# Two-layer graph attention kernel: normalisations of phase A one step later, and the weight and token sums at the boundary shared out anew

## The chip, the cores and the metric

The kernel runs on one core of one Trainium2 chip. The metric is the device time of one execution in microseconds (us), taken as the median of several runs. A separate profiled execution gives the trace: its *span* is the time from the first to the last instruction of the program.

A core has five engines that run their own instruction queues and meet through semaphores: TensorE (PE in the profile, with its weight loads as PEld), VectorE (DVE), ScalarE (ACT), GpSimd (POOL) and SyncE (SP, which here issues all DMAs). Each queue is worked in the order in which the program wrote it.

## The reference, cut to what matters

The input is 128 graphs of 64 nodes with 768 features in float32. Two layers follow each other, each with a residual and a layer normalisation:

```python
# layer 0: gated graph attention with 12 heads of 64
h    = x @ W                       # per head
attn = softmax(mask(leaky(tanh(h) @ w_src + (tanh(h) @ w_dst).T)))
gate = sigmoid(x @ H_w.T + H_b)
x    = layernorm(x + gate * elu(attn @ h + b) + (1 - gate) * x)
# layer 1: masked attention with 6 heads of 128
q, k, v = x @ Wq + bq, x @ Wk + bk, x @ Wv + bv
x    = layernorm(x + softmax(q @ k.T / sqrt(128) + bias) @ v @ Wf + bf)
```

## The kernel before, in words

The 8192 rows make 64 tiles of 128 rows, two graphs each. Two tiles form a pair, and there are 32 pairs (`NP`). All large products are done with fewer multiplications by a scheme in the manner of Strassen: sums of blocks of the tokens and of the weights are made first, on VectorE or GpSimd, and TensorE then multiplies these.

**Phase A** does layer 0 and the product with Wv. A pair takes part in three products, W (for h), G (for the gate) and V (for v). Each consists of seven dense steps `i` = 0 to 6 of three matmuls (`Product.matmuls`, line 209), and after each step one eviction: steps 0, 2 and 3 copy the running sum to a `snap` buffer on ScalarE (line 418), steps 1, 4 and 5 add such a copy on VectorE (lines 441 and 460), step 6 copies on ScalarE (lines 439 and 458). TensorE may go on in the same accumulator only when the eviction has read it: step 4 needs the snap of step 2, step 5 that of step 3, step 6 the addition of step 4.

The order of all work is written out by hand. `at(step, ...)` appends a function to a list of events for a numbered step, and `run` calls them step by step. Within a step the order is that of the appending, where earlier pairs come first. Pair `p` begins at step `O[p]`: 0, 14, 28, and then every 21 steps. From there the attention of its two tiles follows in fixed distances. The object `Tile0(p, 1)` starts at `s = o`, `Tile0(p, 0)` five steps later. In what follows "30.0" is tile 0 of pair 30, and "W4.2" is dense step 2 of the product W of pair 4. The parts of a tile that matter here:

- `add` (ScalarE, line 532), `mask` and `top` (VectorE, lines 539 and 543), `exp` (ScalarE, line 548), `scale` (a reciprocal on VectorE, line 556, then a product on GpSimd, line 558): the softmax.
- `probs` (TensorE transposes, line 569, copied by ScalarE, line 574), `aggregate` (TensorE, line 587), `elu` (lines 608 and 615), `mix1` and `mix2` (VectorE, lines 620 to 630).
- `norm1` (step `s + 29`): statistics on VectorE, then 1/sqrt and a shift on GpSimd (lines 296 to 301). `norm2` (step `s + 30`): the normalisation itself on ScalarE (line 305), which waits for that shift. Only for the last pair is it done on VectorE (line 639). `spill` (step `s + 31`): SyncE stores the tile.
- `load(p)` (step `o + 8`) reads the pair's x into two of the four slots 0, 1, 5 and 6 of the buffer `xb`; the slots were those of pair `p - 2`.
- `x1_in` reads a spilled tile back in blocks, `x1T` transposes it on VectorE (line 397), `x1_sums` makes its token sums on GpSimd, and the product V follows. For the last pair `x1T` is done by TensorE (line 412).

**The boundary.** At the end of phase A the weights of layer 1 are prepared. Wq and Wk are loaded early into the buffers that W and H_w leave. Each needs 14 sums over slots of 128 x 512 elements (`WEIGHT_SUMS`, `weight15_sum`, line 167): VectorE makes those of Wq, GpSimd those of Wk, from step `o + 44` and `o + 45` of the last pair on, beside its V product.

**Phase B** does layer 1 for 16 groups of two pairs. A group first makes q and k for its heads in two halves `j`, in the order q0, k0, q1, k1. Each is a `Stream` of 15 steps (`STEPS`, `R` = 15) of two matmuls (line 876); the half `j` reads only columns `j * 128` to `j * 128 + 127` of each weight slot. ScalarE and VectorE collect the results (lines 897 and 902). The tokens' side needs 11 sums over the group (`SUMS`, `group_sum`, line 846, 128 x 512 each) of the transposed tokens `T4`, which lie in slots 1 to 4 of `xb`. For group 0 all are made on VectorE, four steps ahead of their use or, where that is not possible, before the first step. For group 1 six are made on VectorE and five on GpSimd, for later groups all on GpSimd. `dup` holds copies of four parts of group 0's tokens, made by ScalarE (line 1113), so that `T4` can be refilled. After q and k come scores, softmax, context (`load_v` brings v into slots 5, 6 and 0 of `xb`) and the product with Wf (steps F, from step 150 of the group). Wf is loaded in steps 2 to 7 of phase B, and its 14 sums are made by GpSimd from step 16 on. `load_adj` loads the mask of a group and has VectorE turn it into `fill` at once (line 811).

Of the kernel before, what the change touches and what calls it, by code (L numbers as in the profile page):

```python
# [9 lines left out]
F32 = mybir.dt.float32  # L10
# [51 lines left out]
def kernel(  # L62
# [99 lines left out]
        r = src.rearrange("(h p c) o -> h c p o", h=2, c=CH)  # L162
        return [r[k // CH, k % CH] for k in range(NC)]

    def weight15_sum(wb, k, eng):
        to, a, b, sign = WEIGHT_SUMS[k]
        eng.tensor_tensor(wb[:, to], wb[:, a], wb[:, b], SIGN[sign])

    def weight_sums(part, eng, ks=range(4)):

# [97 lines left out]


    T4 = xb[:, 1:5].rearrange("p (q i) (c n) -> p q i c n", q=2, n=P)  # L270

    def load_T4(g):
        for q in range(2):
# [34 lines left out]
    def phase_a(ctx):  # L308
# [342 lines left out]
        def at(step, *fs):  # L651
            events.setdefault(max(step, 0), []).extend(fs)

        def dense(d, key, i):
            d[key].matmuls(i)
            d[key].evict(i)
# [19 lines left out]
        for p in range(NP):  # L676
            d, o = st[p], O[p]
            d["p"] = p
            if p:
                at(max(o - 20, 1), lambda p=p: load_adj(p))  # L680
                at(o + 8, lambda p=p: load(p))

            def xb_in(d, i):
                d.setdefault("xp", []).append(blocks(x_t[2 * d["p"] + i]))

            def xT(d, i):
                d.setdefault("T", []).append(turn(d["xp"][i]))
# [12 lines left out]
            for i in range(7):  # L700
                at(o + i, lambda d=d, i=i: dense(d, "W", i))
                at(o + 7 + i, lambda d=d, i=i: dense(d, "G", i))
            for i, s in ((1, o), (0, o + (4 if p == NP - 1 else 5))):
                t = Tile0(p, i)
                at(s + 6 + (i == 0), t.tanh, t.cap)
                at(s + 7, t.dst_mul)
                at(s + 8, t.src_mul)
                at(s + 9, t.dst_sum, t.dst_out)
                at(s + 10, t.src_sum)
                at(s + 13, t.dst_in)  # L710
                at(s + 16, t.exchange)

                at(s + (15 if i else 17), lambda t=t: t.add(0))
                at(s + (16 if i else 17), lambda t=t: t.add(1))
                at(o + (14 if i else 16), t.gate_in)
                at(o + (17 if i else 18), t.gate)
                n = s - (i == 1)
                at(n + 18, t.mask, t.top)
                at(n + 19, lambda t=t: t.exp(0))
                at(n + 20, lambda t=t: t.exp(1))  # L720
                at(s + 21, lambda t=t: t.scale(0), lambda t=t: t.scale(1))
                at(s + 24, t.probs)
                at(s + 25, t.aggregate)
                at(s + 26, t.elu)
                at(s + 27, t.mix1)
                at(s + 28, t.mix2)
                at(s + 29, t.norm1)
                at(s + 30, t.norm2)
                at(s + 31, t.spill)

            def x1_in(d, i):
                d["xp", i] = blocks(x1_d[2 * d["p"] + i])

            def x1T(d, i, t):
                d["x1T", i] = t
                nc.sync.dma_start(xT_d[d["p"]][:, i], t)

            def x1_sums(d):
                d["T"] = [d["x1T", i] for i in range(2)]
                sums(d)  # L740

            if p < NP - 3:
                v = O[p + 3] + 14
                times = ((1, v - 19, v - 13), (0, v - 16, v - 10))
            elif p < NP - 1:

                v = O[-1] + (21 if p == NP - 3 else 28)
                times = ((1, v - 16, v - 7), (0, v - 15, v - 6)) if p == NP - 3 else (
                    (1, v - 12, v - 7), (0, v - 10, v - 6)
                )  # L750
            if p < NP - 1:
                for i, t0, t1 in times:
                    at(t0, lambda d=d, i=i: x1_in(d, i))
                    at(t1, lambda d=d, i=i: x1T(d, i, turn(d["xp", i])))
                at(times[1][2] + 1, lambda d=d: x1_sums(d))
            else:
                v = o + 45
                for i in range(2):
                    at(o + 43 - i, lambda d=d, i=i: x1T(d, i, transposed(d["x"][i])))
# [6 lines left out]
            at(4 + c, lambda c=c: weight_sums(lambda s: w1[:, s, c], nc.vector))  # L766


        o = O[-1]
        early = []  # L770

        def load_early(i, src, k):
            if k == 0:
                early.append(weight15(i))
            load15(early[i], src, k)

# [9 lines left out]
        return early  # L786


    def phase_b(ctx, wq, wk):
# [15 lines left out]
        def load_adj(g):  # L805
            d = st[g]
            a = small.tile([P, 2, 2, S], U8, name="adj1")
            for q in range(2):
                nc.sync.dma_start(a[:, q], adj_p[2 * g + q])
            d["fill"] = small.tile([P, 2, 2, S], F32, name="fill1")  # L810
            nc.vector.tensor_scalar(
                d["fill"], a, 1.0, -L1_NEG, op0=ALU.subtract, op1=ALU.mult
            )

        def load_v(g, q, i):
# [18 lines left out]
                nc.gpsimd.tensor_tensor(t, t, bf_bc, ALU.add)  # L834


        def group_part(d, r):

            if r < 6:
                return T4[:, :, r // 3, 2 * (r % 3) : 2 * (r % 3) + 2, :]  # L840
            return d["S"][r - 6]

        def group_sum(d, k, eng):
            r0, r1, op = SUMS[k]
            t = k1.tile([P, 2, 2, P], F32, name=f"S{k}")
            eng.tensor_tensor(t, group_part(d, r0), group_part(d, r1), op)  # L846
            d["S"][k] = t

        def pair_part(d, q, r):

# [217 lines left out]
        def at(step, *fs):  # L1068
            events.setdefault(max(step, 0), []).extend(fs)
# [4 lines left out]

        R = len(STEPS)
        N = 6 * R
        wf = weight15(2)
        for k in range(NC):
            at(2 + k, lambda k=k: load15(wf, Wf, k))
        for k in range(len(WEIGHT_SUMS)):  # L1080
            at(16 + 2 * k, lambda k=k: weight15_sum(wf, k, nc.gpsimd))
        for g in range(NG):
            d, o = st[g], N * g
            d["S"] = {}
# [5 lines left out]
            for k in range(len(SUMS)):  # L1090
# [19 lines left out]
                at(t, lambda d=d, k=k, eng=eng: group_sum(d, k, eng))  # L1110
# [114 lines left out]
```

## Time and profile before

| | |
|---|---|
| median of 3 runs | 2884.05 us (2882.27 to 2884.43) |
| the profiled execution's own time | 2882.71 us |
| its span | 2880.6 us |
| TensorE busy | 2825.0 us, 98% |
| VectorE busy | 1877.8 us, 65% |
| GpSimd busy | 1535.4 us, 53% |
| ScalarE busy | 1201.5 us, 42% |
| mean granted TensorE clock | 0.997 of full speed |

The 2.1 us between span and time lie around the program. A line of the timeline gives start, duration, engine, line of the kernel, operation and names (`out<-in`), the shape and how many instructions it merges; in brackets stand the idle time of the engine before it and what ended that idle time. Matmuls are recorded in pairs: a dense step of phase A is `x6`, one of a stream `x4`. Phase A lies from 0 to some 1470 us, phase B from 1475 us on.

### The profile page before, as it was taken

Reading aid. Unit: us, or ns where it says so; the run is one execution under the profiler, and the core shown is the slowest. Engines: PE = TensorE matmul, PEld = TensorE weight load, DVE = VectorE, ACT = ScalarE, POOL = GpSimd, SP = SyncE. Lnnn points to the kernel's source line nnn. Section 1 sums busy time; section 2 is a strip of 40 time slices with the busy share of each in tenths; the row PEclk is TensorE's granted clock in tenths of the full one; section 3 lists DMA queues with packets and bytes.
Section 4 is the critical chain, followed back from the end, with each engine's and each line's share of the span. In section 5 each row is a group of like instructions: output and inputs, shape, how many; then the busy total and the mean of one; then the engine's idle time right before and its main releaser. Section 6 shows DMA issues by size and latency. Waiting matters only on the chain.

```text
span 2880.6 us, 50750 instructions
## 1 busy us (share of the span) xinstructions
PE 2825.0 (98%) x18108; PEld 2061.9 (72%) x18108; DVE 1877.8 (65%) x3716; ACT 1201.5 (42%) x3737; POOL 1535.4 (53%) x1633
## 2 busy tenths in 40 slices
PE   8899999999999999999989999999999999999998
PEld 4556566666665665666558888888888888888887
DVE  4787777777877777778675555555555555555556
ACT  4656656566566565565522221222211222211223
POOL 4755655655555565555462555346454456454455
PEclk9999999999999999999999999999999999999999
DMA  6335445344454454443640211212211212211222
GB/s 179 108 107 155 126 134 150 116 146 137 124 146 137 124 155 122 139 143 121 201 147 18 89 69 59 84 56 89 89 65 58 89 56 89 89 61 62 89 83 72
DMA packets 358683, 308.40 MB, mean 107 GB/s; under 512 B 226592, under 2 KB 304160, under 8 KB 358432
## 3 DMA queue, kind: packets, MB, share of 16 engines
q1 hardware_dynamic: 358432, 305.16, 34.5%
q8 instruction: 144, 2.36, 0.3%
q14 instruction: 107, 0.88, 0.1%
HBM read 191.41 MB, written 101.06 MB: 102 GB/s over the span
## 4 chain that ended last, share of the span: by engine, by line
PE 86%; DVE 6%; POOL 3%; DMA 2%; issue 1%; ACT 1%; SPq 1%; DVEq 0%; POOLq 0%; ACTq 0%
PE X L876 42%; PE X L209 37%; PE pb L1016 2%; PE pb L941 2%; PE pa L587 2%; PE pa L569 1%; DVE z L629 1%; PE pb L996 1%; DVE z L620 1%; DVE S L846 0%; DVE w L173 0%; POOL th L490 0%; POOL w L173 0%; DVE st L284 0%; DVE xb L630 0%
## 5 line engine op out<-in xcount | busy, mean ns | idle before, releaser
L209 PE MATMUL X<-w,S 128*128 128x384 f32 x2304 | 800.8, 493 | 18.2 <-ACT snap L418 7.4
L876 PE MATMUL X<-S,w 128*128 128x256 f32 x2816 | 667.0, 383 | 7.2 <-DVE S L846 5.9
L209 PEld LDWEIGHTS X<-w,S 128*128 128x128 f32 x2304 | 430.6, 191 | 309.4 <-ACT snap L418 18.4
L209 PE MATMUL X<-w,T 128*128 128x384 f32 x1728 | 596.1, 487 | 6.0 <-ACT snap L418 3.5
L876 PEld LDWEIGHTS X<-S,w 128*128 128x128 f32 x2816 | 525.5, 190 | 82.2 <-DVE S L846 7.3
L209 PEld LDWEIGHTS X<-w,T 128*128 128x128 f32 x1728 | 326.1, 191 | 229.4 <-ACT snap L418 7.8
L858 POOL TENSOR_TENSOR Sc<-cT 128x256 f32<-128x256 f32 x224 | 161.7, 729 | 405.4 <-PE X L876 392.0
L876 PE MATMUL X<-w,Sc 128*128 128x256 f32 x1408 | 322.5, 381 | 0.9 <-DVE xs L919 0.8
L919 DVE TENSOR_TENSOR xs<-xs,X 128x256 f32<-128x256 f32 x512 | 210.6, 420 | 169.0 <-PE X L876 160.3
L876 PEld LDWEIGHTS X<-w,Sc 128*128 128x128 f32 x1408 | 265.4, 190 | 38.7 <-DVE xs L919 1.6
L548 ACT ACTIVATE s<-s,nmx 128x64 f32<-128x64 f32 x768 | 256.2, 335 | 76.8 <-DVE nmx L543 76.8
L902 DVE TENSOR_TENSOR k<-k,X 128x256 f32<-128x256 f32 x320 | 133.7, 421 | 216.0 <-PE X L876 166.1
L902 DVE TENSOR_TENSOR q<-q,X 128x256 f32<-128x256 f32 x320 | 133.2, 420 | 179.7 <-PE X L876 146.0
L305 ACT ACTIVATE xs<-xs,shift,rstd 128x768 f32<-128x768 f32 x62 | 63.5, 1025 | 419.0 <-POOL shift L301 412.4
L876 PE MATMUL X<-xb,w 128*128 128x256 f32 x960 | 236.6, 379 | 0.0
L897 ACT ACTIVATE k<-X,bk_c 128x256 f32<-128x256 f32 x192 | 91.1, 474 | 306.9 <-PE X L876 306.8
L897 ACT ACTIVATE q<-X,bq_c 128x256 f32<-128x256 f32 x192 | 91.1, 474 | 284.3 <-PE X L876 284.3
L482 POOL TENSOR_TENSOR tmp<-th,wd_bc 128x768 f32<-128x768 f32 x64 | 141.4, 2210 | 126.8 <-ACT th L478 126.8
L296 POOL TENSOR_TENSOR rstd<-rstd,neg_half 128x1 f32<-128x1 f32 x126 | 69.3, 550 | 247.4 <-DVE rstd L295 246.3
L532 ACT ACTIVATE s<-s,src 128x64 f32<-128x64 f32 x768 | 193.3, 335 | 15.0 <-DMA s<-dst_d 14.4
L876 PEld LDWEIGHTS X<-xb,w 128*128 128x128 f32 x960 | 181.2, 190 | 24.0
L418 ACT COPY snap<-X 128x384 f32<-128x384 f32 x288 | 134.8, 468 | 101.3 <-PE X L209 99.5
(119 smaller groups left out, 4110.3 us busy)
## 6 DMA issues: line engine op xcount, KB each, us to landing
xb<-in_x_dram SPq DMA_DIRECT2D x64, 384.0 KB
s<-dst_d SPq DMA_DIRECT2D x128, 192.0 KB
x_d<-xb SPq DMA_DIRECT2D x64, 384.0 KB
xT_d<-T SPq DMA_DIRECT2D x64, 384.0 KB
v_d<-v SPq DMA_DIRECT2D x128, 192.0 KB
xb<-xT_d SPq DMA_DIRECT2D x32, 768.0 KB
xb<-v_d SPq DMA_DIRECT2D x256, 96.0 KB
xs<-x_d SPq DMA_DIRECT2D x64, 384.0 KB
```

Source lines behind the costliest of these rows:

```text
L209: nc.tensor.matmul(o, self.lhsT(i, c), rhs, start=first and c == 0, stop=last and c == CH - 1, skip_group_check=True,)
L296: nc.gpsimd.tensor_tensor(rstd, rstd, neg_half, ALU.pow)
L305: nc.scalar.activation(r, r, AF.Identity, bias=shift, scale=rstd)
L418: nc.scalar.copy(t, ps)
L482: nc.gpsimd.tensor_tensor(self.tmp, self.th, wd_bc, ALU.mult)
L532: nc.scalar.activation(self.s[:, a], self.s[:, a], AF.Prelu, bias=self.src[:, a : a + 1], alpha=LEAKY_ALPHA,)
L548: nc.scalar.activation(self.s[:, a], self.s[:, a], AF.Exp, bias=self.nmx[:, a : a + 1], accum_out=self.sm[:, a : a + 1],)
L858: nc.gpsimd.tensor_tensor(t, pair_part(d, q, r0), pair_part(d, q, r1), op)
L876: nc.tensor.matmul(ps, self.lhsT(r, slot, c), self.rhs(r, slot, c), start=start and c == 0, stop=stop and c == 1, skip_group_check=True,)
L897: nc.scalar.activation(o[:, b], ps, AF.Identity, bias=bias[:, hd : hd + 1], scale=1.0 if positive else -1.0)
L902: nc.vector.tensor_tensor(o[:, b], o[:, b], ps, ALU.add if positive else ALU.subtract)
L919: nc.vector.tensor_tensor(o, o, ps, ALU.add if positive else ALU.subtract)
```

## The change

1. In phase A, `norm2` and `spill` of all pairs but the last come one step later. `load(p)` moves from `o + 8` to `o + 10`. `scale` of tile 1 is put at the front of its step. For pair 30, `x1_in` of tile 1 is one step earlier and both `x1T` (and the sums after them) one step later.
2. `weight15_sum` takes a range of columns. At the boundary VectorE makes only the first 128 of the 256 columns of each of the two blocks in a slot, so 128 x 256 elements a sum: all 14 of Wq in steps `o + 44` to `o + 47`, and the first 9 of Wk in `o + 49` to `o + 51`. Between them, at `o + 48`, it makes the first four group sums of group 0, into slots of `xb` that x has left (0, 5 and 6).
3. In phase B VectorE makes Wk's last five first halves in steps 8 to 12. GpSimd makes the first sum of Wf in step 8, then the second halves of Wq (steps 9 to 22) and of Wk (21 to 34), and the other 13 sums of Wf in steps 68 to 92. At the end of phase A GpSimd makes no weight sums any more.
4. Group 0's other seven sums stay on VectorE, in the order of their need, five steps ahead. Group 1's eleven sums are all on GpSimd, one step later than before.
5. The `fill` of a group is no longer made with the load of its mask, but in step 26 of the group.

```diff
-    def weight15_sum(wb, k, eng):
+    def weight15_sum(wb, k, eng, o=slice(0, 256)):
         to, a, b, sign = WEIGHT_SUMS[k]
-        eng.tensor_tensor(wb[:, to], wb[:, a], wb[:, b], SIGN[sign])
+        eng.tensor_tensor(wb[:, to, :, o], wb[:, a, :, o], wb[:, b, :, o], SIGN[sign])
...
+    free = [xb[:, 0], *(xb[:, 5:7].rearrange("p t (u n) -> p (t u) n", u=3)[:, 2 * k : 2 * k + 2] for k in range(3))]
+    EARLY = [free[0].rearrange("p (u n) -> p u n", u=3)[:, :2], *free[1:]]
+    EARLY = [t.rearrange("p q (c n) -> p q c n", n=P) for t in EARLY]
+    WK_EARLY = 9
...
+    def group_sum(d, k, eng, t):
+        r0, r1, op = SUMS[k]
+        eng.tensor_tensor(t, group_part(d, r0), group_part(d, r1), op)
+        d["S"][k] = t
...
+        def at_front(step, *fs):
+            events.setdefault(step, [])[:0] = fs
...
-                at(o + 8, lambda p=p: load(p))
+                at(o + 10, lambda p=p: load(p))
...
-                at(s + 21, lambda t=t: t.scale(0), lambda t=t: t.scale(1))
+                (at_front if i else at)(s + 21, lambda t=t: t.scale(0), lambda t=t: t.scale(1))
...
-                at(s + 30, t.norm2)
-                at(s + 31, t.spill)
+
+                n = s + (0 if p == NP - 1 else 1)
+                at(n + 30, t.norm2)
+                at(n + 31, t.spill)
...
-                    (1, v - 12, v - 7), (0, v - 10, v - 6)
+                    (1, v - 13, v - 6), (0, v - 10, v - 5)
...
-            at(o + 44 + k // 2, lambda k=k: weight15_sum(early[0], k, nc.vector))
-            at(o + 45 + k // 2, lambda k=k: weight15_sum(early[1], k, nc.gpsimd))
+            at(o + 44 + k // 4, lambda k=k: weight15_sum(early[0], k, nc.vector, slice(0, P)))
+        for k in range(4):
+            at(o + 48, lambda k=k: group_sum(early_sums, k, nc.vector, EARLY[k]))
+        for k in range(WK_EARLY):
+            at(o + 49 + k // 3, lambda k=k: weight15_sum(early[1], k, nc.vector, slice(0, P)))
...
+            d["adj"] = a
+
+        def fill(d):
             d["fill"] = small.tile([P, 2, 2, S], F32, name="fill1")
...
-        for k in range(len(WEIGHT_SUMS)):
-            at(16 + 2 * k, lambda k=k: weight15_sum(wf, k, nc.gpsimd))
+        for k in range(WK_EARLY, len(WEIGHT_SUMS)):
+            at(8 + (k - WK_EARLY), lambda k=k: weight15_sum(wk, k, nc.vector, slice(0, P)))
+
+        at(8, lambda: weight15_sum(wf, 0, nc.gpsimd))
+        for n, wb in enumerate((wq, wk)):
+            for k in range(len(WEIGHT_SUMS)):
+                at(9 + 12 * n + k, lambda wb=wb, k=k: weight15_sum(wb, k, nc.gpsimd, slice(P, 2 * P)))
+        for k in range(1, len(WEIGHT_SUMS)):
+            at(66 + 2 * k, lambda k=k: weight15_sum(wf, k, nc.gpsimd))
...
+            at(o + 26, lambda d=d: fill(d))
...
-                eng = nc.vector if g == 1 and k in (2, 3, 5, 6, 8, 10) else nc.gpsimd
...
-                    t = max(min(SUM_STEPS[k], *(
-                        [SUM_STEPS[m] - 1 for m in range(len(SUMS)) if 6 + k in SUMS[m][:2]] or [99]
-                    )) - 4, -1)
-                    if t < 0:
-                        group_sum(d, k, nc.vector)
-                    else:
-                        at(t, lambda d=d, k=k: group_sum(d, k, nc.vector))
+                    if k > 3:
+                        at(max(int(need(k)) - 5, 0), lambda d=d, k=k: sum_of_group(d, k, nc.vector))
...
-                    t = max([R * 3 + SUM_STEPS[k] + 1] + [ready[r] for r in SUMS[k][:2] if r in ready])
+                    t = max([R * 3 + SUM_STEPS[k] + 2] + [ready[r] for r in SUMS[k][:2] if r in ready])
```

`need(k)` is the step at which sum `k`, or a sum made from it, is first used.

More of the change, by code (lines that the diff above doesn't have):

```diff
@@ L270, with group_part @@
     T4 = xb[:, 1:5].rearrange("p (q i) (c n) -> p q i c n", q=2, n=P)
+    free = [xb[:, 0], *(xb[:, 5:7].rearrange("p t (u n) -> p (t u) n", u=3)[:, 2 * k : 2 * k + 2] for k in range(3))]
+    EARLY = [free[0].rearrange("p (u n) -> p u n", u=3)[:, :2], *free[1:]]
+    EARLY = [t.rearrange("p q (c n) -> p q c n", n=P) for t in EARLY]
+    WK_EARLY = 9
+    def group_part(d, r):
+        if r < 6:
+            return T4[:, :, r // 3, 2 * (r % 3) : 2 * (r % 3) + 2, :]
+        return d["S"][r - 6]
+    def group_sum(d, k, eng, t):
+        r0, r1, op = SUMS[k]
+        eng.tensor_tensor(t, group_part(d, r0), group_part(d, r1), op)
+        d["S"][k] = t
     def load_T4(g):
@@ L766, in phase_a @@
             at(4 + c, lambda c=c: weight_sums(lambda s: w1[:, s, c], nc.vector))
+        early_sums = {"S": {}}
         o = O[-1]
@@ L772, in load_early @@
         def load_early(i, src, k):
-            if k == 0:
+            if len(early) == i:
                 early.append(weight15(i))
@@ L780, in phase_a, with phase_b @@
         for k in range(len(WEIGHT_SUMS)):
-            at(o + 44 + k // 2, lambda k=k: weight15_sum(early[0], k, nc.vector))
-            at(o + 45 + k // 2, lambda k=k: weight15_sum(early[1], k, nc.gpsimd))
+            at(o + 44 + k // 4, lambda k=k: weight15_sum(early[0], k, nc.vector, slice(0, P)))
[3 more added lines that the diff above has]
+            at(o + 49 + k // 3, lambda k=k: weight15_sum(early[1], k, nc.vector, slice(0, P)))
         at(o + 30, lambda: load_T4(0))
         run(events, O[-1] + 80)
-        return early
-    def phase_b(ctx, wq, wk):
+        return *early, early_sums["S"]
+    def phase_b(ctx, wq, wk, early_sums):
         NG = NP // 2
@@ L809, in load_adj @@
                 nc.sync.dma_start(a[:, q], adj_p[2 * g + q])
+            d["adj"] = a
+        def fill(d):
             d["fill"] = small.tile([P, 2, 2, S], F32, name="fill1")
             nc.vector.tensor_scalar(
-                d["fill"], a, 1.0, -L1_NEG, op0=ALU.subtract, op1=ALU.mult
+                d["fill"], d["adj"], 1.0, -L1_NEG, op0=ALU.subtract, op1=ALU.mult
             )
@@ L834, in add_bf, with sum_of_group @@
                 nc.gpsimd.tensor_tensor(t, t, bf_bc, ALU.add)
[L837 to L847, printed above, removed]
+        def sum_of_group(d, k, eng):
+            group_sum(d, k, eng, k1.tile([P, 2, 2, P], F32, name=f"S{k}"))
         def pair_part(d, q, r):
@@ L1076, in phase_b, with need @@
         N = 6 * R
+        def need(k):
+            return min([SUM_STEPS[k]] + [
+                need(m) - 0.5 for m in range(len(SUMS)) if 6 + k in SUMS[m][:2]
+            ])
         wf = weight15(2)
@@ L1079, in phase_b @@
             at(2 + k, lambda k=k: load15(wf, Wf, k))
-        for k in range(len(WEIGHT_SUMS)):
-            at(16 + 2 * k, lambda k=k: weight15_sum(wf, k, nc.gpsimd))
+        for k in range(WK_EARLY, len(WEIGHT_SUMS)):
[6 more added lines that the diff above has]
+            at(66 + 2 * k, lambda k=k: weight15_sum(wf, k, nc.gpsimd))
         for g in range(NG):
             d, o = st[g], N * g
-            d["S"] = {}
+            d["S"] = {} if g else early_sums
             last = g == NG - 1
@@ L1088, in phase_b @@
                 at(o - 35, lambda g=g: load_adj(g))
+            at(o + 26, lambda d=d: fill(d))
             ready = {}
-            for k in range(len(SUMS)):
-                eng = nc.vector if g == 1 and k in (2, 3, 5, 6, 8, 10) else nc.gpsimd
+            for k in sorted(range(len(SUMS)), key=need) if g == 0 else range(len(SUMS)):
                 if g == 0:
-                    t = max(min(SUM_STEPS[k], *(
-                        [SUM_STEPS[m] - 1 for m in range(len(SUMS)) if 6 + k in SUMS[m][:2]] or [99]
-                    )) - 4, -1)
-                    if t < 0:
-                        group_sum(d, k, nc.vector)
-                    else:
-                        at(t, lambda d=d, k=k: group_sum(d, k, nc.vector))
+                    if k > 3:
+                        at(max(int(need(k)) - 5, 0), lambda d=d, k=k: sum_of_group(d, k, nc.vector))
                     continue
                 if g == 1:
-                    t = max([R * 3 + SUM_STEPS[k] + 1] + [ready[r] for r in SUMS[k][:2] if r in ready])
+                    t = max([R * 3 + SUM_STEPS[k] + 2] + [ready[r] for r in SUMS[k][:2] if r in ready])
                     ready[6 + k] = t
@@ L1109, in phase_b @@
                     t = o - 24 + 2 * k
-                at(t, lambda d=d, k=k, eng=eng: group_sum(d, k, eng))
+                at(t, lambda d=d, k=k: sum_of_group(d, k, nc.gpsimd))
             if g == 0:
```

## The prediction

> **What bounds the kernel now.** I read the page's busy shares first, then busy time by stage, then TensorE's waits, and then the queues at the two places where it waits.
>
> ```profile
> PE 2825.0 (98%) x18108; PEld 2061.9 (72%) x18108; DVE 1877.8 (65%) x3716; ACT 1201.5 (42%) x3737; POOL 1535.4 (53%) x1633
> ```
>
> TensorE is the bound. The change takes no matmul away, so only its 55.6 us of idle time and its slow clock can be won. Where they lie (length, then busy time of PE, PEld, DVE, ACT, POOL, then the clock):
>
> ```profile
> 60.00:200.00 140.00, 123.63 (x750) 72.14 (x749) 108.68 (x162) 93.85 (x348) 91.56 (x82) 0.96 0.38 111
> 200.00:540.00 340.00, 340.00 (x1752) 204.55 (x1742) 258.15 (x404) 212.60 (x738) 194.69 (x186) 1.00 0.46 135
> ...
> 1380.00:1475.00 95.00, 82.61 (x401) 48.36 (x399) 73.54 (x99) 40.76 (x134) 53.60 (x47) 0.98 0.59 185
> 1475.00:1540.00 65.00, 59.44 (x340) 49.66 (x341) 36.96 (x71) 11.38 (x24) 30.68 (x22) 0.97 0.28 83
> 1540.00:2800.00 1260.00, 1259.94 (x9670) 1090.74 (x9669) 685.65 (x1809) 274.90 (x530) 621.62 (x759) 1.00 0.22 74
> ```
>
> 16.4 us are idle between 60 and 200 us (the first pairs, 14 steps apart), 18.0 us between 1380 and 1540 us (the boundary); the long stretches are full. TensorE's waits (total, times, longest):
>
> ```profile
> PE X L209 <- ACT snap L418: 10.9, 6, 3.6
> ...
> PE X L876 <- DVE S L846: 5.9, 4, 4.1
> PE X L209 <- DVE v L460: 3.5, 3, 2.6
> ```
>
> The first line belongs to the first pairs. ScalarE's timeline shows why:
>
> ```profile
> 83.83 1.54 ACT L532 ACTIVATE s<-s,src 128x64 f32<-128x64 f32 x6
> 90.05 1.03 ACT L305 ACTIVATE xb<-xb,shift,rstd 128x768 f32<-128x768 f32 x1 [4.68 <-POOL shift L301]
> 90.99 1.53 ACT L532 ACTIVATE s<-s,src 128x64 f32<-128x64 f32 x6
> 92.42 0.46 ACT L418 COPY snap<-X 128x384 f32<-128x384 f32 x1
> ```
>
> norm2 of 0.1 stands idle 4.68 us for GpSimd's shift. Behind it wait the second half of an add and the snap of W2.2, and TensorE stands 2.64 us. At the boundary VectorE is late (its timeline, then TensorE's):
>
> ```profile
> 1457.93 9.16 DVE L167 TENSOR_TENSOR w<-w 128x512 f32<-128x512 f32 x6
> 1467.01 0.55 DVE L460 TENSOR_TENSOR v<-X,snap 128x384 f32<-128x384 f32 x1
> ```
> ```profile
> 1467.70 3.74 PE L209 MATMUL X<-w,S 128*128 128x384 f32 x6 [2.60 <-DVE v L460]
> 1475.50 3.40 PE L876 MATMUL X<-S,w 128*128 128x256 f32 x8 [4.06 <-DVE S L846]
> ```
>
> Six weight sums hold V31.4's eviction back, then group sums hold the first stream back. After both waits the matmuls are slow too: 3.74 us against 2.10 for six.
>
> [...] line 167 on VectorE has 677 ns at least and 1502 ns as median while GpSimd runs its own. [...] TensorE's clock record has five such windows between 60 us and the boundary's end (after the waits of 2.64, 3.63, 3.28, 2.60 and 4.06 us), each costing some 1.6 us (3.74 - 2.10).
>
> **The boundary, step by step.** V31.0 begins at 1453.22, a dense step takes 1.94. VectorE is free at 1451.9. Wq's halves: GpSimd's token sums for pair 31 run until 1456.9, so I give the first eight 0.75 each (half of 1502), to 1457.9; V31.1's eviction 0.55 (ready at 1457.1); six halves alone at 0.37 ([...] 0.42 long additions of 256 start 0.33 apart) to 1460.7; four group sums at 0.65 to 1463.3. V31.4 ends at 1463.0, its eviction at 1463.9. V31.6 wants it at 1465.1, so TensorE does not wait and ends at 1467.1, not 1471.4: 4.3 won (2.60 and 1.64 of clock). Behind this come three Wk halves, V31.5's eviction, six more: 1468. Then sums 4 to 6: 1468.7, 1469.3, 1470.0. A stream step takes 0.866; steps 4 and 5 want them at 1470.6 and 1471.4. So the 4.06 and its 1.4 of clock (3.40 against 1.97) go. One new wait: the four copies to `dup` (2.18 us on ScalarE, from 1467.5) now stand before step 0's collection, due at 1469.7 for step 3: 0.5 lost.
>
> In phase B the waits of 0.84, 0.21, 0.47 and 0.55 for sums and q go, since the sums are ahead. The wait of 1.06 at 1498.61 goes: VectorE's `fill` stood 4.15 us for the mask's load, with k's additions behind it; in step 26 the mask has long landed. The waits of 1.49 and 0.45 near 1536 go: six group sums (0.6 to 0.7 each) in VectorE's queue delayed k's last additions, and these are GpSimd's now. Sum: 4.3 + 5.5 + 5.1 - 0.5 = 14.4.
>
> What was moved and counted at nothing: Wf's six loads follow V31's stores and one bias load on SP, so now issue from 1468.4; from first issue to first sum it was 9.0 us before (1472.86 to 1481.87), so GpSimd starts at 1477.4, in step 12. Its Wf sum (1.6 at most) and 14 halves of Wq (0.73 alone, as line 858 for 128 x 256) end at 1489 to 1490. q1 starts at 1493.1 and wants only the sixth by its second step. Wk's halves end by 1501 (k1: 1506). If this cover fails, each us late costs one. Wk's last five halves are VectorE's in steps 8 to 12, before k0 in step 15. The other Wf sums (13 x 1.27 to 1.6, steps 68 to 92) precede F in step 150. Group 1's eleven sums (14 us of GpSimd from step 47) precede step 90. v's loads now wait on SP until slots 5, 6 and 0 are read for the last time (step 54): used in step 108; only later loads queue behind. The evictions from PSUM stay at 0.42 beside GpSimd, as they did at 1500.
>
> **Phase A.** Later norm2 lets add and snap go first. At W2.4 (ready 90.29) the snap is there. The next snap, W2.3's, is behind norm2 (90.05), elu's exp and a tanh: 0.94 + 0.84 + 0.74 + 0.46 put its end at 93.1. So W2.5 starts at 93.1, not 96.47: 3.4 won, of which add, mask and exp of tile 1.0, and G2.3's snap behind them, leave 2.8 at 112. At W3.4 (3.63 and clock) the same way gives 6 and leaves 4.9 at 151. V0.5's 3.12 goes, but VectorE is busy without a break from 153.8 to 171.6, so V0.4's eviction, 4.9 earlier, holds V0.6: still 4.9. At W4.2 (3.28, named for GpSimd's `s`, which ended last; the snap of W4.0 behind norm2 explains it) the wait and its clock go, and scale of 3.0, ready 2.2 before its use at 196.5, leaves about 7. I take 6.5. After 200 us TensorE is full, and norm2 one snap later only relaxes the queue. x loads two steps later are used in step `o + 27`. Pair 30's order moves mask 31.0 at 1423.40 ahead by 0.3, with 2.8 of the 3.13 at 1428.8 staying. The front place of scale passes only one weight sum of 1.0 at 66 us: nothing.
>
> Total: 14.4 + 6.5 + 0.3 = 21.2. The profiled execution took 2882.71 (span 2880.6, 2.1 around it): 2861.5. The median lies 1.3 higher: 2862.8.
>
> **Bounds and rivals.** A half could cost between 0.34 (half of 0.68) and 0.68 (all fixed); I take 0.37. At 0.68, VectorE's sum 4 would come 2 to 3 us late with one slow window: 4 back.
>
> - *Forecast* (0.55): 2859 to 2867.
> - *Phase A's waits only move* (0.22): its chain through VectorE, busy 108.7 of 140 us, is the limit; 1 to 3 won there, 2867.5.
> - *They go altogether* (0.12): the five snap waits between 90 and 170 us, the one at 181.57 and three slow windows, 13.6 + 5, of which some 13 stay: 2856.
> - *The halves cost like whole sums* (0.08): speaks for it the fixed part, against it the 0.42 additions; 10 at the boundary and 3 to 6 before: 2868 to 2871.
> - *Slower* (0.03): GpSimd, held by Wf's load, makes Wq's second halves too late for q1. Its sixth instruction is done 9 us before the need. Each us past that costs one, so it decides when Wf lands 30 us later than I say: 2890 at 36 late. Against it: 9.0 us for this load now.
>
> The bound of a measurable change is 0.2%, 5.8 us. All but the last case are beyond it. The 8 in 10 range takes in the second, most of the third and part of the fourth case: 2856 to 2871.
>
> **What would show it.** Right: line 305 no longer before a late snap, and idle between 60 and 200 us down from 16.4 to some 10; line 167 on VectorE near 0.4 us; V31.6 without wait, the first stream step straight behind it; no waits near 1498 and 1536; clock windows at the boundary gone. Wrong: line 167 at 0.7 or more, TensorE waiting for line 167 on GpSimd in q1, or new waits in the 44 us period after 200 us, where each 0.75 us in 28 pairs would eat all.

## The result and the profile after

| | before | after |
|---|---|---|
| median of 6 runs | 2883.57 us (2880.62 to 2885.85) | 2873.22 us (2871.92 to 2875.11) |
| profiled execution, its span | 2882.71, 2880.6 us | 2871.92, 2870.1 us |

The ratio of the times is 0.9965 (0.9952 to 0.9978). The change makes the kernel faster by about 10 us. The forecast was 2862.8 us (2856 to 2871): the direction is right, but the gain is half of what was forecast and the time lies 2.2 us above the range.

The page's busy shares for the kernel after:

```profile
PE 2823.4 (98%) x18108; PEld 2062.7 (72%) x18108; DVE 1862.2 (65%) x3724; ACT 1200.4 (42%) x3737; POOL 1546.7 (54%) x1653
```

TensorE has the same number of matmuls and nearly the same busy time. Its idle time fell from 55.6 to 46.7 us. Where it lies now, by the same stretches (length, then busy time of PE, PEld, DVE, ACT, POOL, then the clock):

```profile
60.00:200.00 140.00, 126.11 (x767) 74.07 (x766) 113.63 (x173) 97.45 (x354) 97.10 (x86) 0.99 0.38 107
200.00:540.00 340.00, 339.92 (x1785) 204.47 (x1784) 255.38 (x397) 213.26 (x756) 195.88 (x185) 1.00 0.48 140
...
1380.00:1475.00 95.00, 89.11 (x442) 56.02 (x441) 73.91 (x126) 40.29 (x124) 33.56 (x33) 1.00 0.63 205
1475.00:1540.00 65.00, 58.91 (x353) 51.21 (x351) 29.24 (x70) 13.29 (x28) 51.73 (x54) 0.98 0.15 47
1540.00:2800.00 1260.00, 1259.02 (x9657) 1090.03 (x9658) 679.65 (x1797) 273.25 (x526) 622.31 (x759) 1.00 0.22 74
```

Between 1380 and 1475 us, 12.4 us of idle time became 5.9, and the clock is full. Between 1475 and 1540 us nothing was won: 6.1 us are idle and the clock is 0.98. TensorE's waits show what is there (total, times, longest):

```profile
PE pb L1016 <- POOL s L1010: 6.9, 1, 6.9
PE X L209 <- ACT snap L434: 5.5, 6, 2.0
...
PE X L209 <- DVE v L476: 3.0, 2, 2.5
PE X L209 <- DVE hp L457: 2.9, 1, 2.9
```

The snap waits fell from 10.9 to 5.5 us, and the waits for the first group sums left the head of the list. In front stands one wait that the kernel before does not have: the transposes of group 0's probabilities (line 1016) wait 6.9 us for GpSimd's product with 1/sum (line 1010), the softmax's scale.

Since the matmuls are the same in both kernels, the same matmul can be looked up in both traces. The table gives how much earlier it starts in the kernel after:

| place in the program (time in after) | earlier by, us | what lies between |
|---|---|---|
| start of phase A (70) | -0.5 | 1.0 ahead at 18 us behind the first loads, then a half-speed window at 21.8 us |
| probabilities of pair 4 (197) | 4.85 | 5.4 won in the first pairs |
| the same, end of the steady stage (1387) | 2.36 | 2.5 lost in small pieces |
| last aggregate (1436) | 3.05 | 0.7 won at pair 30 |
| first stream step of group 1 (1519.83) | 19.2 | 16.2 won at the boundary |
| first probabilities of group 0, past the wait (1545) | 10.45 | 8.8 lost |

It stays at 10.4 to the end, beside 10.5 us between the spans.

**The boundary gain.** VectorE's timeline, of after:

```profile
1448.79 5.29 DVE L167 TENSOR_TENSOR w<-w 128x256 f32<-128x256 f32 x8
1454.41 0.56 DVE L476 TENSOR_TENSOR v<-X,snap 128x384 f32<-128x384 f32 x1 [0.33 <-PE X L209]
1454.89 2.59 DVE L167 TENSOR_TENSOR w<-w 128x256 f32<-128x256 f32 x6
1457.39 2.62 DVE L285 TENSOR_TENSOR xb<-xb 128x512 f32<-128x512 f32 x4
1460.22 0.56 DVE L476 TENSOR_TENSOR v<-X,snap 128x384 f32<-128x384 f32 x1 [0.20 <-PE X L209]
```

Six half sums take 2.59 us where six whole ones took 9.16, so V31.4's eviction waits for TensorE and no longer the other way round. TensorE's own timeline:

```profile
1461.90 2.10 PE L209 MATMUL X<-w,S 128*128 128x384 f32 x6
1463.83 1.89 PE L896 MATMUL X<-xb,w 128*128 128x256 f32 x8
...
1467.02 1.13 PE L896 MATMUL X<-xb,w 128*128 128x256 f32 x4 [0.43 <-ACT q L917]
```

V31.6 has no wait, six matmuls take 2.10 us instead of 3.74, and the first stream step follows straight behind. The one wait left, 0.43 us, is the one that the forecast laid to the `dup` copies.

**The new wait.** GpSimd's timeline, of after:

```profile
1474.48 22.61 POOL L167 TENSOR_TENSOR w<-w 128x512 f32<-128x512 f32 x29 [20.68 <-DMA w<-in_L_gnn_Wf_dram]
...
1509.69 1.27 POOL L285 TENSOR_TENSOR S<-xb 128x512 f32<-128x512 f32 x1 [10.14 <-PE X L896]
...
1522.46 17.54 POOL L167 TENSOR_TENSOR w<-w 128x512 f32<-128x512 f32 x13
1539.95 1.62 POOL L1010 TENSOR_TENSOR s<-s,rs 128x384 f32<-128x384 f32 x2
```

and TensorE's beside it:

```profile
1532.89 1.03 PE L896 MATMUL X<-S,w 128*128 128x256 f32 x4
1540.84 0.90 PE L1016 MATMUL pb<-ident,s 128*128 128x128 f32 x3 [6.92 <-POOL s L1010]
1541.53 1.91 PE L896 MATMUL X<-S,w 128*128 128x256 f32 x4
```

GpSimd first makes Wf's one sum and all second halves (ended at 1497.1) and two of group 1's sums. Then it stands 10.14 us until TensorE has read what the next of these overwrites, makes the other nine, and then all 13 other sums of Wf in one piece. Only behind these comes the scale of group 0's softmax. VectorE had its 1/sum ready at 1532.3:

```profile
1532.13 0.18 DVE L1009 RECIPROCAL rs<-sm 128x6 f32<-128x6 f32 x1
```

So the scale lay ready for 7.6 us behind sums that nobody wanted before step 150. In steps 60 to 89 TensorE has only group 0's last scores to make (step 62), so on the engines step 92 follows almost at once on step 59: putting the sums in "steps 68 to 92" gave them no time of their own. The record of the clock shows two half-speed windows of 3.41 us in a row, from 1537.4 to 1544.2. The second begins as TensorE resumes (x4 takes 1.91 us and not 1.03) and costs 1.7 us. 6.9 and 1.7 are 8.6 of the 8.8.

**The first pairs.** ScalarE's timeline, of after:

```profile
89.00 0.48 ACT L434 COPY snap<-X 128x384 f32<-128x384 f32 x1 [1.58 <-PE X L209]
90.67 1.03 ACT L321 ACTIVATE xb<-xb,shift,rstd 128x768 f32<-128x768 f32 x1 [1.19 <-POOL shift L317]
...
93.17 0.46 ACT L434 COPY snap<-X 128x384 f32<-128x384 f32 x1
```

The snap of W2.2 is taken at 89.00 ahead of norm2, not behind it at 92.42, and norm2 idles 1.19 us, not 4.68. Half-speed windows at 92.6, 130.1 and 181.3 us before became one at 134.5. The stretch from 60 to 200 us is not as empty of waits as forecast (13.9 us idle, not some 10): 2.9 us for `hp` and 2.5 for `v` on VectorE are there now.

### The profile page after: what moved, and what is told of

It is laid out like the page before. It is cut to its first block, busy times and chain, and to the rows that moved or that the text cites. A ratio compares the mean times of both kernels' runs of the same rounds, so it can differ in the third digit from the quotient of the medians.

```text
span 2870.1 us, 50797 instructions
## 1 busy us (share of the span) xinstructions
PE 2823.4 (98%) x18108; PEld 2062.7 (72%) x18108; DVE 1862.2 (65%) x3724; ACT 1200.4 (42%) x3737; POOL 1546.7 (54%) x1653
## 3 DMA queue, kind: packets, MB, share of 16 engines
q8 instruction: 144, 2.36, 0.3%
## 4 chain that ended last, share of the span: by engine, by line
PE 85%; DVE 6%; POOL 3%; DMA 2%; ACT 2%; issue 1%; SPq 1%; DVEq 0%; POOLq 0%; ACTq 0%
PE X L896 42%; PE X L209 36%; PE pb L1036 2%; PE pb L961 2%; PE pa L603 1%; DMA s<-dst_d 1%; PE pa L585 1%; PE pb L1016 1%; DVE z L645 1%; ACT s L548 1%; POOL w L167 1%; ACT s L564 1%; DVE s L555 1%; DVE z L636 1%; DVE w L173 0%
## 5 line engine op out<-in xcount | busy, mean ns | idle before, releaser
L896 PE MATMUL X<-S,w 128*128 128x256 f32 x2752 | 651.3, 382 | 0.0
L896 PEld LDWEIGHTS X<-S,w 128*128 128x128 f32 x2752 | 513.6, 190 | 70.1
L209 PEld LDWEIGHTS X<-w,T 128*128 128x128 f32 x1728 | 325.5, 191 | 233.7 <-ACT snap L434 16.2
L896 PE MATMUL X<-xb,w 128*128 128x256 f32 x1024 | 253.1, 380 | 0.4 <-ACT q L917 0.4
L498 POOL TENSOR_TENSOR tmp<-th,wd_bc 128x768 f32<-128x768 f32 x64 | 147.5, 2305 | 130.5 <-ACT th L494 107.6
L896 PEld LDWEIGHTS X<-xb,w 128*128 128x128 f32 x1024 | 193.7, 190 | 26.9 <-ACT q L917 0.8
```

The source lines that it names most:

```text
L209: nc.tensor.matmul(o, self.lhsT(i, c), rhs, start=first and c == 0, stop=last and c == CH - 1, skip_group_check=True,)
L498: nc.gpsimd.tensor_tensor(self.tmp, self.th, wd_bc, ALU.mult)
L896: nc.tensor.matmul(ps, self.lhsT(r, slot, c), self.rhs(r, slot, c), start=start and c == 0, stop=stop and c == 1, skip_group_check=True,)
```

## The experiments

Two things had to be explained: the new wait, which costs most, and the 2.5 us that are lost again in the steady stage of phase A. Then whether the parts add up, and what bounds the first pairs.

### Wf's sums elsewhere in GpSimd's queue

`wf_early` puts eight of the 13 sums into steps 37 to 44, where GpSimd had stood for 10.14 us, and the last five into steps 62 to 66:

```diff
-            at(66 + 2 * k, lambda k=k: weight15_sum(wf, k, nc.gpsimd))
+            at(36 + k if k < 9 else 53 + k, lambda k=k: weight15_sum(wf, k, nc.gpsimd))
```

> The changed kernel, with the last 13 sums of Wf moved on GpSimd: eight of them to steps 37 to 44, ahead of group 1's sums, in the 10.1 us in which GpSimd stood idle there, the other five to steps 62 to 66. Theory (queue): group 0's first softmax product on GpSimd (line 1010) came 7 us late because 17.5 us of Wf sums stood directly ahead of it; steps 60 to 89 hold no matmuls, so steps 68 to 92 gave no time. Then GpSimd is done with the sums before 1532 us, TensorE's wait of 6.92 us and its slow clock of some 1.7 us go, and the time falls from 2873.2 to 2864.6 us (2863.5 to 2866). Rival (softmax itself): the probabilities come late because VectorE's chain for group 0 is late, whatever GpSimd does; then the time stays within 1 us of 2873.

`wf_late` puts them behind the scale, before Wf is used:

```diff
-            at(66 + 2 * k, lambda k=k: weight15_sum(wf, k, nc.gpsimd))
+            at(114 + 2 * k, lambda k=k: weight15_sum(wf, k, nc.gpsimd))
```

> The changed kernel, with the last 13 sums of Wf moved behind the softmax of group 0, to steps 116 to 140, still ahead of their first use in step 150. Theory (queue): as with the early place, the wait of 6.92 us goes and the time is 2864.6 us (2863.5 to 2868, as these sums now stand between the pair sums that the product with Wf needs, and may cost it up to 3 us). Rival (GpSimd has too much work between 1474 and 1534 us in any order): not told apart by this run alone from the queue theory, but a time near 2873 would speak against both.

`wf_three_late` leaves ten where they are and moves only the last three, 4.0 us of work, behind the scale:

```diff
-            at(66 + 2 * k, lambda k=k: weight15_sum(wf, k, nc.gpsimd))
+            at(66 + 2 * k if k < 11 else 94 + 2 * k, lambda k=k: weight15_sum(wf, k, nc.gpsimd))
```

> The changed kernel, with only the last three of Wf's 13 sums moved behind the softmax (steps 116 to 120), as a dose. Theory (queue): each sum takes 1.35 us on GpSimd in that stretch (17.54 us for 13), so the scale on GpSimd starts 4.0 us sooner and TensorE's wait shrinks from 6.92 to 2.9 us; the half-speed clock behind it falls away or is halved (0 to 1.7 us). Time 2869.2 us, or 2867.5 without slow clock. If the wait has a threshold (some other work that the sums collide with), it stays near 6.9 or goes altogether (2873 or 2864.6).

Measured: `wf_early` 2865.79 us (2863.61 to 2869.02), ratio to the kernel before 0.994 (0.9924 to 0.9957); `wf_late` 2866.98 us (2863.84 to 2869.08), 0.994 (0.9925 to 0.9955). In both the wait at line 1016 is gone. GpSimd's timeline, of `wf_early`:

```profile
1522.90 6.73 POOL L167 TENSOR_TENSOR w<-w 128x512 f32<-128x512 f32 x5
1532.90 0.83 POOL L1010 TENSOR_TENSOR s<-s,rs 128x384 f32<-128x384 f32 x1 [3.27 <-DVE rs L1009]
```

The scale now waits for its 1/sum, and not the 1/sum for the scale. `wf_three_late` left this wait of TensorE:

```profile
PE pb L1016 <- POOL s L1010: 3.0, 1, 3.0
```

4.0 us of sums taken out of the queue shorten the wait by 3.9. That the scale's place behind these sums makes the wait is thus shown three ways, moving them ahead, moving them back, and by dose.

The time of `wf_three_late`, 2872.31 us (2871.21 to 2873.31; 0.9962, 0.9947 to 0.9977), is some 3 us longer than expected. In its profiled execution the wait is as short as forecast, but phase A lost 4.1 us in the steady stage, 1.6 more than the profile of after. That stage is the subject of the third group of runs. Two half-speed windows come on top, at 1428.6 and 1452.5 us, that the profile of after does not have. With them its matmuls are 4.5 us behind those of after at group 1's first stream step.

### Each part of the change alone

`phase_a_only` is the kernel before with item 1 of the change; `boundary_only` is the kernel after with item 1 undone:

```diff
-                n = s + (0 if p == NP - 1 else 1)
+                n = s
...
-                at(o + 10, lambda p=p: load(p))
+                at(o + 8, lambda p=p: load(p))
...
-                (at_front if i else at)(s + 21, lambda t=t: t.scale(0), lambda t=t: t.scale(1))
+                at(s + 21, lambda t=t: t.scale(0), lambda t=t: t.scale(1))
...
-                    (1, v - 13, v - 6), (0, v - 10, v - 5)
+                    (1, v - 12, v - 7), (0, v - 10, v - 6)
```

> The kernel before, with the edits of phase A alone (norm2 and spill one step later, loads of x two steps later, scale of tile 1 in front, pair 30's order). The trace of the changed kernel shows its phase A ahead by 5.4 us at pair 4, by 2.4 us at 1388 us and 3.0 us at 1436 us. Theory: this alone gives 2880.6 us (2879.5 to 2882), that is 2 to 4 us less than before. Rival, the prediction as it stood: 6.8 us less, 2876.8.

> The changed kernel with the edits of phase A undone (norm2, spill, loads, scale and pair 30 as before). Theory: the boundary gives 16.2 us up to group 1's first step, and the softmax wait takes 8.6 back: 2883.6 - 7.6 = 2876.0 us (2875 to 2877.5). If phase A and boundary weaken each other, the two single runs add up to more than the 10.3 us of both together.

Measured: `phase_a_only` 2882.01 us (2878.57 to 2883.75), ratio 0.9994 (0.9985 to 1.0002). `boundary_only` 2874.87 us (2872.28 to 2879.46), 0.9968 (0.9957 to 0.998), a little under what was expected. The part in phase A, from which the forecast took 6.8 us, brings 1.5 on the medians (-0.6 to 4.3 by the interval of the ratio). Its trace has the gain at 197 us, where the matmuls are 6.25 us ahead (0.8 of it from the start of the program), but at 1387 us only 1.22 are left. `boundary_only` has the wait of 6.9 us at line 1016 as well, so that belongs to the boundary's part.

`boundary_wf_early` is `boundary_only` with the sums of Wf where `wf_early` has them:

> The boundary alone (phase A as before), with Wf's sums early. Theory: 2883.6 - 16.2 = 2867.4 us (2866 to 2869), the whole of the boundary's gain with no wait in the softmax. The prediction had 14.4, that is 2869.2.

Measured: 2867.87 us (2865.79 to 2871.55), 0.9948 (0.9933 to 0.9963). So without its own new wait the boundary is worth 16.1 us on the medians (2883.93 to 2867.87). That fits the 16.2 of the comparison of the traces, but the interval of the ratio (10.7 to 19.3 us) holds the 14.4 of the forecast too.

### What eats the gain in the steady stage

In the profile of after the losses come in a dozen places, 0.05 to 0.5 us each, nearly all at W.5. The SP queue, which issues all DMAs, shows a possible cause. The same stretch of the pair's period before and after (start, time to issue, line, names):

```profile
303.60 0.38 SPq L647 DMA_DIRECT2D x_d<-xb  x1
305.62 2.58 SPq L390 DMA_DIRECT2D xp<-x_d  x4
...
310.41 1.19 SPq L508 DMA_DIRECT2D s<-dst_d  x2
```
```profile
300.75 2.58 SPq L406 DMA_DIRECT2D xp<-x_d  x4
303.44 0.55 SPq L663 DMA_DIRECT2D x_d<-xb  x1
...
306.20 1.14 SPq L524 DMA_DIRECT2D s<-dst_d  x2
```

The change moves `spill` by a step together with `norm2`. Before, the store was issued at 303.60, in a gap of the queue ahead of four loads. After, it stands behind these loads, which start at the same place (300.75 + 4.85 = 305.60), and the load of `s` that feeds the softmax comes 0.64 us late (306.20 + 4.85 = 311.05, against 310.41). Rival: ScalarE, where norm2 now stands one snap later, delays the snap that W.5 needs. The test leaves norm2 late and issues the spill where it was:

```diff
-                at(n + 31, t.spill)
+                at(n + (31 if p == NP - 1 else 30), t.spill)
```

`spill_at_norm` is the kernel after with this edit, `phase_a_spill` is `phase_a_only` with it:

> The changed kernel, with the spill of all pairs but the last in the same step as its (late) norm2, so that SP issues it ahead of the x1_in of an older pair and not behind it. Seen in the trace: phase A is 4.85 us ahead at pair 4 and 2.4 at 1388 us, lost in small waits of 0.05 to 0.76 us at W.5 of a pair, and the load of s for tile 0 goes out 0.6 us later after its pair's V step than before. Theory (SP queue): the spill stands on SP behind four loads and puts the exchange and the load of s behind itself; with the order mended these waits go, phase A keeps its 4.85 us, and the time falls by 2.4 us to 2870.8 (2870 to 2872). Rival (ScalarE queue): norm2 itself, one step later, delays the snap of W.3; then the small waits stay and the time is 2873.2.

> The kernel before, with phase A's edits alone and the spill in the step of its norm2. Theory (SP queue): some 5 us ahead at pair 4 and still so at 1388 us, without the small waits at W.5; the time is 2.4 us less than with phase A's edits as they are (2882.0), 2879.6 (2878 to 2881). Rival: no difference, 2882.

Measured: `spill_at_norm` 2871.39 us (2870.1 to 2873.57), ratio 0.9957 (0.9942 to 0.9972); `phase_a_spill` 2877.76 us (2875.02 to 2880.31), 0.9978 (0.997 to 0.9985), 0.2 us better than its range and 4.2 us below `phase_a_only`, where the rival said 2882. The 1.8 us between `spill_at_norm` and after are less clear, as the ranges of their times overlap; there the traces decide. How far ahead of the kernel before the matmuls are at the two ends of the steady stage, for every kernel with item 1 of the change:

| kernel | spill | at 197 us | at 1387 us | change |
|---|---|---|---|---|
| after | late | 4.85 | 2.36 | -2.5 |
| `wf_early` | late | 6.61 | 2.84 | -3.8 |
| `wf_late` | late | 5.03 | 0.99 | -4.0 |
| `wf_three_late` | late | 5.00 | 0.92 | -4.1 |
| `phase_a_only` | late | 6.25 | 1.22 | -5.0 |
| `lite_after` (further down) | late | 12.14 | 6.44 | -5.7 |
| `spill_at_norm` | with norm2 | 3.76 | 3.51 | -0.3 |
| `phase_a_spill` | with norm2 | 6.49 | 7.08 | +0.6 |
| `both` (further down) | with norm2 | 4.58 | 4.56 | 0.0 |

Every kernel with the late spill loses 2.5 to 5.7 us; with the spill a step earlier, and norm2 as late as in the others, none loses more than 0.3. `boundary_only` and `boundary_wf_early`, with item 1 undone, change by -0.3 and +0.7. So norm2's later place on ScalarE costs next to nothing there, and the spill's place in SP's queue costs the 2.5 to 5.7.

The traces point to the load of `s` as the way by which it reaches W.5. From 200 to 1380 us ScalarE's `add` stands idle 9.9 us for this load in the kernel before and 9.1 in `phase_a_spill`, but 25.7 in after and 28.3 in `phase_a_only`. One pair in `phase_a_only`, ScalarE and then TensorE:

```profile
1239.67 2.97 ACT L532 ACTIVATE s<-s,src 128x64 f32<-128x64 f32 x12 [1.64 <-DMA s<-dst_d]
...
1246.72 0.46 ACT L418 COPY snap<-X 128x384 f32<-128x384 f32 x1
```
```profile
1247.23 2.20 PE L209 MATMUL X<-w,T 128*128 128x384 f32 x6 [0.52 <-ACT snap L418]
```

The same pair in `phase_a_spill`, where W.5 does not wait:

```profile
1233.64 2.97 ACT L532 ACTIVATE s<-s,src 128x64 f32<-128x64 f32 x12 [0.28 <-DMA s<-dst_d]
...
1240.69 0.46 ACT L418 COPY snap<-X 128x384 f32<-128x384 f32 x1
```

Mask and maximum on VectorE follow the add, and the snap stands on ScalarE behind six of the exps that wait for these. Whether the delayed exchange of `hx` has a share in other pairs was not told apart.

### Both mended

`both` is the kernel after with the edits of `wf_early` and `spill_at_norm`:

> The changed kernel with both mends: Wf's sums early as in the run that took 2865.8 us, and the spill in the step of its norm2. If the two are independent, 2863.4 us (2862 to 2865). If the spill's place is without effect, 2865.8.

Measured: 2861.38 us (2859.21 to 2862.54), ratio to the kernel before 0.9921 (0.9904 to 0.9937), a bit better than expected and faster than both kernels of this case. Its windows in the places of the two losses:

```profile
540.00:1380.00 840.00, 839.79 (x4454) 506.06 (x4453) 637.03 (x993) 523.95 (x1825) 479.32 (x458) 1.00 0.46 135
1380.00:1475.00 95.00, 89.12 (x446) 56.64 (x445) 74.38 (x125) 39.49 (x122) 34.33 (x34) 1.00 0.66 211
1475.00:1540.00 65.00, 65.00 (x468) 56.50 (x470) 29.50 (x75) 16.24 (x35) 52.04 (x55) 1.00 0.14 40
```

From 1475 to 1540 us TensorE is busy throughout at the full clock. The matmuls are 4.58 us ahead at 197 us and still 4.56 at 1387. The parts add up on the medians: 6.2 for phase A with its spill mended and 16.1 for the boundary with its sums mended make 22.3, and `both` gains 22.8. That is closer than the spread of single runs (3 to 6 us in each kernel) would promise.

### What bounds the first pairs

The second rival of the forecast said that VectorE's chain limits the first pairs, so that the later norm2 brings little. The test takes VectorE work away there, in both kernels: the minimum and maximum of the ELU are left out for the first four pairs, so that part of the result is missing.

```diff
-                nc.vector.scalar_tensor_tensor(z, e, 1.0, z, op0=ALU.min, op1=ALU.max)
+                if self.p >= 4:
+                    nc.vector.scalar_tensor_tensor(z, e, 1.0, z, op0=ALU.min, op1=ALU.max)
```

> The changed kernel, with the first operation of mix1 (minimum and maximum of the ELU, line 636, 1.0 to 2.5 us each) left out for pairs 0 to 3; that part of the ELU is missing there. Theory (VectorE's chain limits the first pairs, so that waits for a snap turn into waits for an addition on VectorE): with some 1.5 us less on VectorE per tile, the waits of 2.9 us for hp and 2.6 us for v on VectorE shrink below 1 us, and phase A at pair 4 is ahead of the kernel before by 9 us or more, where the changed kernel is ahead by 5. Rival (GpSimd's or the DMAs' chain is the limit): the waits pass to GpSimd's scale or the load of s, and it stays within 1.5 us of 5.

> The kernel before, with the same operation of mix1 left out for pairs 0 to 3 (line 620). Here norm2 on ScalarE stands ahead of the snap; its shift comes from VectorE's statistics, so less work on VectorE shortens the same waits, but not to nothing: 2 to 6 us ahead of the kernel before at pair 4, and the snap waits of ScalarE stay the largest ones. If VectorE's chain is not the limit, less than 1.5 us.

Measured, one run each: 2869.06 us for `lite_after`, 2877.64 for `lite_before`. At pair 4 they are 12.14 and 7.10 us ahead of the kernel before; 0.5 and 0.9 of this come from the start of the program. For the second, 2 to 6 had been expected. TensorE's wait for VectorE's `v`, of `lite_after`, and the largest of `lite_before`:

```profile
PE X L209 <- DVE v L476: 1.9, 2, 1.4
```
```profile
PE X L209 <- ACT snap L418: 7.2, 7, 2.9
```

The waits for `v` and `hp` shrank to 1.4 and 1.2 us at the longest, not below 1 as expected. Without what comes from the start, the two are 11.6 and 6.2 us ahead, so the later norm2 is worth 5.4 us with less work on VectorE; with all of it, it is 5.4 too. In these single profiles both limits are real and nearly independent: taking an operation of 0.95 to 1.66 us per tile from VectorE brings 6.2 us with or without the change. The rival named a limit that is there, but it doesn't swallow the gain.

## Why the prediction was right and where it was wrong

The sum was 14.4 + 6.5 + 0.3 = 21.2; the spans differ by 10.5.

- **Failed step: "The other Wf sums (13 x 1.27 to 1.6, steps 68 to 92) precede F in step 150", counted at nothing.** It cost 8.8 us. The working asked only who uses these sums. It did not ask what stands behind them on GpSimd, the scale of group 0's softmax in step 102, nor whether steps 68 to 92 take any time. They take almost none on TensorE; group 1's sums had been shifted to the same place, so 14 us of them and 17.5 of Wf's met. The runs showed it by moving the sums both ways and by moving three.
- **Failed step: "After 200 us TensorE is full, and norm2 one snap later only relaxes the queue", counted at nothing.** It cost 2.5 us in the profile of after, up to 5.7 in others. ScalarE was indeed no problem. The spill that moves along was not followed onto SP's queue, where one step puts it behind four loads that take 2.58 us together.
- **The boundary, 14.4: right in mechanism, short in size, 16.2.** Half sums at 0.41 to 0.43 (0.37 was taken), V31.6 and the first stream without wait, 0.43 for `dup` (0.5), no waits near 1498 and 1536: as forecast. The first eight halves took 0.66 on average (0.75 was taken), but as five alone at 0.41 and three beside GpSimd at 1.10 to 1.22. A whole sum alone took 0.68 us in the kernel before, so half the columns saved 0.25 to 0.27 us and not 0.34. What is missing is in the way waits were read: each of the small waits of 0.21 to 1.49 us that went saved up to 0.26 us more than its idle time, when the same matmuls are compared in both traces. TensorE's record has x4 last 1.03 us while the next begins 0.87 after it, so 0.16 of a wait is hidden, and the first matmul behind most of them takes another 0.10. Over nine waits this makes the 1.8. The 16.2 holds where no half-speed window falls into this stretch, as the forecast assumed (after, `both`, `lite_after`). In the profiles of the six other kernels with this part of the change one falls at 1448 to 1454 us, and the stretch gives 14.9.
- **Phase A's first pairs, 6.5: right in mechanism, 5.4 in size.** The snaps moved ahead of norm2 as described. New waits for `hp` (2.9 us with its slow clock behind it) and `v` (2.5) stayed for VectorE, which the forecast had made the rival and not a deduction. Pair 30 gave 0.7 for 0.3. The five slow windows that the forecast counts do follow the waits that it lists, of 2.60 to 4.06 us; that its length alone did not decide, the last section shows.
- **Wf's load and Wq's second halves: right.** The first sum starts at 1474.48 (1477.4 had been said, on a clock three us behind this one), all halves are done by 1497.1, and no matmul of q1 or k1 waits for them. The slower case did not come near.

The measured time lies close to the case "the halves cost like whole sums" (2868 to 2871), but not for its reason. With both failed steps mended the kernel takes 2861.38, beside the forecast of 2862.8: a wait it left out and a queue it did not follow, less 1.8 that was undercounted, make most of the error. That the two come so close is in part luck, since 1.8 too little at the boundary and 1.1 too much in the first pairs cancel.

## What to carry to other kernels

When work is moved on an in-order queue, "it is used much later" is half of the check: list also what stands behind it on that queue and when this is ready (here a scale that lay ready for 7.6 us, with TensorE waiting 6.9). A step number in a hand-written schedule is an order, not a time, so count which engine works in the steps between. A store that is moved with its producer moves on the DMA queue too, and one step may put it behind a batch of loads (here four, 2.58 us, with the load behind it 0.64 us late); the total time shows this as a gain that trickles away, which comparing the start of the same matmul in both traces makes visible.

## What the runs showed of the hardware beyond that

- Half-speed windows did not follow from the length of a wait alone: in the kernel before, waits of 2.60 and 2.64 us were followed by one, while waits of 3.12 and 3.13 (at 169.61 and 1428.81 us) were not. The clock records of before and after fit another measure. Up to 2850 us each half-speed stretch lasts 3.41 us, or 6.83 in the one case of two in a row, and within each trace they start whole multiples of 3.413 us apart (before: 92.58, 130.12 and 181.32 us, 11 and 15 windows apart). With both traces cut into this grid from 30 to 2850 us, a full-speed window was followed by a half-speed one 7 times, with 2.29 to 3.41 us without a matmul in it, and by a full-speed one 1635 times, with at most 1.94. In the kernel before, the grid cut the wait of 3.12 us into 1.2 and 1.9 and that of 3.13 into 1.5 and 1.6, and left the 2.60 whole. A half-speed window was followed by full speed in the seven cases where it had at most 0.52 us without a matmul, and by another in the one where it had 3.41, the wait of 6.9 us in after.
- The grid lies differently against the program in the two profiled executions: from the window at 92.58 us in before to that at 134.48 in after it is 12.28 windows, not a whole number. So by this measure the same wait could be cut in one and left whole in the other. At pair 30, before and after have no half-speed window, `wf_three_late` has one (at 1428.6 us).
- An elementwise sum of 128 x 256 beside GpSimd's sums took 0.61 to 1.47 us on VectorE in after, against 0.41 to 0.43 alone. In before, the ten of 128 x 512 beside GpSimd's weight sums took 0.80 to 1.75 us, the first two, with GpSimd idle, 0.68.
- The start of phase A differs between profiled executions. In after, the matmuls are 1.0 us ahead of before at 18 us, behind the first loads, and 0.5 behind at 70 us, past the half-speed window at 21.84; `lite_before` was 0.9 ahead. Differences of a few us between two single profiles have to be taken from a place behind that.
